# Layer 0 of a two-layer kernel: the second and third weight load of layer 1 issued by ScalarE behind the norm, and the queries' PSUM evictions moved from VectorE to ScalarE

## Chip, cores and metric

One Trainium2 chip, one core. The metric is the device time of one execution in microseconds (us). Engines: PE is TensorE (matrix multiplies; PEld is its weight load), DVE is VectorE, ACT is ScalarE, POOL is GpSimd, SP is SyncE, which here does nothing but ask for transfers. Each engine works through its own instructions in the order in which they were issued and waits on semaphores for the others. PE writes its results into eight PSUM banks, from which DVE or ACT must fetch ("evict") them before the bank can be used again. A transfer (DMA) is asked for by an instruction in one engine's order and carried out by 16 DMA engines beside all of that.

## What is computed

Two layers on x of 4 batches, 256 tokens, 512 features, float32. Each layer norms x and adds an attention-like and a feed-forward branch to it. The change lies in layer 0:

```python
def _L0_attn_ref(x, ...):            # 32 heads, 4 latent numbers a head
    C_q = x @ Wq_d + bq_d            # 512 -> 12
    C_kv = x @ Wkv_d + bkv_d         # 512 -> 4
    q = (C_q @ W_qk + b_qk).reshape(b, s, 32, 4)
    scores = jnp.einsum('bqhd,bkd->bhqk', q, C_kv) / jnp.sqrt(4)
    attn = jax.nn.softmax(scores, axis=-1)
    V = (C_kv @ Wv_u + bv_u).reshape(b, s, 32, 16)
    ...
    return out @ Wo + bo

def _L0_ffn_ref(x, W_gate, W_up, W_down):      # M = 1792
    h = silu(x @ W_gate.T) * (x @ W_up.T)
    return h @ W_down.T

x = x + _L0_attn_ref(xn, ...) + _L0_ffn_ref(xn, ...)
```

Layer 1 norms the new x and adds a selective scan (its input projection `in_proj_w` is 512 x 2048) and a routed feed-forward.

## The kernel before

The order of the work is written out by hand. The feed-forward of layer 0 is a generator (`gate_up`, then `down`): each `yield` is one small step of matmuls, and `go(ff, n)` lets n steps of it run. The attention's steps are called between such `go`s, so that PE has feed-forward matmuls to do while DVE and ACT work on the attention. Tokens go in two halves `th` of 512 (batches 0 and 1, then 2 and 3).

**Feed-forward.** `gate_up(th)` goes over 14 blocks m of 128 hidden features. For each it asks, through GpSimd's queue (L427), for the 256 KB of weights needed three steps on (`wgu`, four buffers), and makes `pg` (gate) and `pu` (up) by 8 matmuls each (L444), since x is held as a high and a low part (`xhi`, `xlo`). ACT makes tanh of `pg` (L451), DVE makes `g` from it (L452) and multiplies by `pu` (L454), ACT rounds that to `hhi` (L455), GpSimd makes the rest `hlo` (L456). `down(th, i)` adds up one block of 128 output tokens in the bank `po`: first the attention's part (L464), from `o8n` and `m_att`, then the hidden features (L469).

**Queries.** `latents(b)` is a generator run for batches 0 and 1 together, later for 2 and 3. It makes the latent numbers of q and k, then `pq`, the queries of 128 (head, latent) rows by 2 x 256 (L310), which is evicted with bias and factor into `q` (L314), rounded to `qhi` by ACT (L319); DVE makes the rest `qlo` (L320). Then 4 times `pqg` by a selection matrix (L335), evicted into `qg` (L337). `scores_max` makes trial scores `sc` (L352) from `qg` and keys `km`, and DVE takes their row maxima `mpl` (L354) out of PSUM. Later `attend` makes exponentials and `weigh` sums them into `av`.

**Norm.** `normalize(b)` copies the sums out of `av` as `o8` (ACT), spreads the denominators over the rows in the bank `pden` (L407), and in four pieces takes the reciprocal (L413) and multiplies (L414) into `o8n`, all on DVE.

**PSUM.** `pg`, `pu`, `po`, `pq`, `pqg`, `pden` take turns in the banks of one pool, so each waits until the one before it in the same bank was read.

**End of layer 0.** After the attention of batch 3 the pool `we` is opened. `w_in` has three buffers of 512 KB for layer 1's input projection; the helper `weights` (L619 to L621) asks SP for such a load. The first is asked for when the pool opens, then `vec`, and two more in the loop over the pieces of `normalize(3)`, which are interleaved with the last two hidden blocks. SP has nothing else to do there and waits for nothing. These loads are for L753 (`px`, layer 1). After `go(ff)` the last `down`s follow, and layer 1 begins.

Of the kernel before, what the change touches and what calls it, by code (L numbers as in the profile page):

```python
# [8 lines left out]
F32 = mybir.dt.float32  # L9

F32R = mybir.dt.float32r
AF = mybir.ActivationFunctionType
ALU = mybir.AluOpType
# [4 lines left out]
P = 128  # L18
# [4 lines left out]
NH, KVL, QL = 32, 4, 12  # L23
# [18 lines left out]
def block_kernel(  # L42
# [24 lines left out]
    nc = tc.nc  # L67
# [5 lines left out]
    x = keep.tile([P, NTB, D], F32, name="x")  # L73
# [28 lines left out]
    ap1 = att.enter_context(tc.tile_pool(name="att", bufs=1, side="right"))  # L102
# [6 lines left out]
    blat = ap1.tile([P, 3], F32, name="blat")  # L109
# [24 lines left out]
    selk = ap1.tile([40, P], F32R, name="selk")  # L134
    ks = ap1.tile([40, S], F32R, name="ks")
    mask = ap1.tile([P, 8], F32, name="mask")


    zk = ap1.tile([P, NTB, 56], F32, name="zk")
# [2 lines left out]
    for i in range(2):  # L142
        t = ap1.tile([P, 2, 4, 32], F32, name=f"mpl{i}")
# [23 lines left out]
    def masks():  # L167
        nc.vector.tensor_reduce(
            mask, ident.rearrange("p (h r) -> p r h", h=4)[:, 16:24, :], AX.X, ALU.add
        )  # L170
        nc.vector.tensor_scalar_mul(mask, mask, -1.0)

    def fold_load():
        live["wvt"] = ffn.tile([P, 4, P], F32, tag="g", name="wvt", bufs=2)
        nc.sync.dma_start(live["wvt"], wvt_d)
        live["wo"] = ap1.tile([P, 4, D], F32, tag="pe", name="wo", bufs=2)
        nc.sync.dma_start(live["wo"], wo_d)
        nc.sync.dma_start(bo, bo_d)
# [107 lines left out]
    def latents(b):  # L286

        xnT = tok[b // 2][0][:, :, b % 2 * S : (b % 2 + 1) * S]
        pl = psmm.tile([P, 2, S], F32, tag="mm", name="pl")
        for hc in range(HC):  # L290
            mm(pl[:40, 0, :], lhsT=wlat[:, hc, :], rhs=xnT[:, hc, :],
               start=(hc == 0), stop=(hc == HC - 1))
        kT = ap1.tile([8, S], F32, tag="kT", name="kT")
        nc.scalar.activation(kT, pl[32:40, 0, :], AF.Identity, bias=blat[32:40, 2:3])
        nc.scalar.copy(ks[0:8, :], kT)
        nc.vector.tensor_tensor(ks[32:40, :], kT, ks[0:8, :].bitcast(F32), ALU.subtract)
        cq = ap1.tile([P, 512], F32, tag="rd", name="cq")[:QL, 0:S]
        nc.scalar.activation(cq, pl[:QL, 0, :], AF.Identity, bias=wqk[:, 0:1])
        yield
        yield  # L300

        kms[b] = ap1.tile([P, S], F32R, tag="km", name="km", bufs=2)
        p = psmm.tile([P, S], F32, tag="mm", name="pkm")
        mm(p, lhsT=selk, rhs=ks, start=True, stop=True)
        nc.scalar.copy(kms[b], p)
        yield
        pq = psmm.tile([P, 2, S], F32, tag="mm", name="pq")
        q8 = ap1.tile([P, 2, S], F32, tag="q8", name="q8")
        for hf in range(2):
            mm(pq[:, hf, :], lhsT=wqk[:, 1 + hf * P : 1 + (hf + 1) * P], rhs=cq,  # L310
               start=True, stop=True)
        for hf in range(2):

            nc.vector.tensor_scalar(  # L314
                q8[:, hf, :], pq[:, hf, :], blat[:, hf : hf + 1], 1.0 / KVL**0.5,
                ALU.add, ALU.mult,
            )
        part = [ap1.tile([P, 2, S], F32R, tag=f"q{n}", name=f"q{n}") for n in ("hi", "lo")]
        nc.scalar.copy(part[0], q8)  # L319
        nc.vector.tensor_tensor(part[1], q8, part[0].bitcast(F32), ALU.subtract)  # L320
        yield


        pz = psmm.tile([P, 2, P], F32, tag="mm", name="pz")
        for i in range(2):
            mm(pz[:, i, :], lhsT=kT[:, i * P : (i + 1) * P], rhs=ident[0:8, :], start=True, stop=True)
        nc.vector.tensor_copy(zk[:, 2 * b : 2 * b + 2, 24:32], pz[:, :, 0:8])
        yield
        qg = ap1.tile([P, 4, 2, S], F32R, tag="qg", name="qg", bufs=2)
        qs[b] = qg  # L330
        for gq in range(4):
            p = psmm.tile([P, 2, S], F32, tag="mm", name="pqg")
            for hf in range(2):
                for k in range(2):
                    mm(p[:, hf, :], lhsT=selq[:, gq, 4 - 4 * k : 4 - 4 * k + P],  # L335
                       rhs=part[k][:, hf, :], start=(k == 0), stop=(k == 1))
            (nc.scalar.copy if gq % 2 else nc.vector.tensor_copy)(qg[:, gq], p)  # L337
            yield


# [60 lines left out]
    def normalize(b):  # L401

        o8 = ffn.tile([P, 2, S], F32, tag="o8", name="o8")
        nc.scalar.copy(o8, avs[b])
        yield
        pd = psmm.tile([P, 2, S], F32, tag="mm", name="pden")
        mm(pd.rearrange("p a b -> p (a b)"), lhsT=rep, rhs=o8.rearrange("p a b -> p (a b)"),  # L407
           start=True, stop=True)
        rd = ffn.tile([P, 2, S], F32, tag="rd", name="rd")
        yield  # L410
        for i in range(4):
            w = slice(i * S // 4, (i + 1) * S // 4)
            nc.vector.reciprocal(rd[:, :, w], pd[:, :, w])  # L413
            nc.vector.tensor_tensor(  # L414
                o8ns[b // 2][:, :, b % 2 * S + i * S // 4 : b % 2 * S + (i + 1) * S // 4],
                o8[:, :, w], rd[:, :, w], ALU.mult,
            )
            yield
# [11 lines left out]
    def gate_up(th):  # L430


        hi, lo = hids[th]
        xs = tok[th][1]
        for m in range(MC):
            for k in range(2):
                i = th * NW + 2 * m + k
                load_w(i + 3)
                if th == 0 and k == 0 and m % 2 == 1:
                    nc.gpsimd.dma_start(wd[:, m - 1 : m + 1, :], wd_d[:, m - 1 : m + 1, :])  # L440
                ps = psmm.tile([P, 512], F32, tag="mm", name="pg" if k == 0 else "pu")
                for hc in range(HC):
                    for j in range(2):
                        mm(ps, lhsT=wgus[i][:, hc, :], rhs=xs[j][:, hc, :],  # L444
                           start=(hc == 0 and j == 0), stop=(hc == HC - 1 and j == 1))
                    if hc < HC - 1:
                        yield

                if k == 0:
                    g = ffn.tile([P, 512], F32, tag="g", name="g", bufs=2)  # L450
                    nc.scalar.activation(g, ps, AF.Tanh, scale=0.5)  # L451
                    nc.vector.scalar_tensor_tensor(g, g, 1.0, ps, ALU.add, ALU.mult)  # L452
                else:
                    nc.vector.scalar_tensor_tensor(g, g, 0.5, ps, ALU.mult, ALU.mult)  # L454
                    nc.scalar.copy(hi[:, m, :], g)  # L455
                    nc.gpsimd.tensor_tensor(lo[:, m, :], g, hi[:, m, :].bitcast(F32), ALU.subtract)  # L456
                yield

    def down(th, i):

        tb = 4 * th + i
        po = psmm.tile([P, D], F32, tag="mm", name="po")
        for hf in range(2):
            mm(po, lhsT=o8ns[th][:, hf, i * P : (i + 1) * P], rhs=m_att[:, hf, :],  # L464
               start=(hf == 0), stop=False)
        yield
        for m in range(MC):
            for j in range(2):
                mm(po, lhsT=hids[th][j][:, m, i * P : (i + 1) * P], rhs=wd[:, m, :],  # L469
                   start=False, stop=(m == MC - 1 and j == 1))  # L470
            if m < MC - 1 or th:
                yield
        if tb < 5:
            nc.vector.tensor_tensor(x[:, tb, :], x[:, tb, :], po, ALU.add)
        else:
            live["last", tb] = po
        yield
# [5 lines left out]
    def go(gen, n=1000):  # L483
        for _ in range(n):
            if next(gen, 1) == 1:
                break
# [64 lines left out]
    ff = gate_up(0)  # L551
# [22 lines left out]
    norm = normalize(0)  # L574
# [7 lines left out]
    norm = normalize(1)  # L582
    next(norm)
    go(ff)
    ff = (0 for i in range(4) for _ in down(0, i))
# [22 lines left out]
    ff = gate_up(1)  # L608
    attention(2, ff, True, 6)
    norm = normalize(2)  # L610
# [5 lines left out]

    we = ctx.enter_context(tc.tile_pool(name="we", bufs=1, side="right"))

    def weights(d, c0):  # L619
        t = we.tile([P, 2, HC, P], F32, tag="w_in", name="w_in", bufs=3)  # L620
        nc.sync.dma_start(t, d[:, c0 : c0 + 2])  # L621
        return t

    w_of = {("x", 0, 0): weights(inx_d, 0)}
# [5 lines left out]
    norm = normalize(3)  # L630
    next(norm)
    go(ff, 4)
    for i, _ in enumerate(norm):
        go(ff, 2)
        if i in (1, 3):
            w_of["x", 0, i // 2 + 1] = weights(inx_d, i + 1)
    go(ff)
    ffs.close()
    ps0.close()

# [40 lines left out]
    for i in range(2):  # L681
        t = w1.tile([P, 2, KC - 1 + S], F32, name=f"pad{i}")
# [421 lines left out]
    ff = (0 for i in range(4) for _ in down(1, i))  # L1104
# [18 lines left out]
    for i in range(2):  # L1123
        v = vec[:, 6 + i, :]
        nc.scalar.activation(px[:, i, :], px[:, i, :], AF.Identity, bias=v[:, V_CB : V_CB + 1],
                             scale=v[:, V_CW + KC - 1 : V_CW + KC])
# [341 lines left out]
```

## Time and profile before

| | us |
|---|---|
| runs | 854.57, 855.86, 847.67, 852.38 (median 853.47) |
| the profiled execution | 852.83 |
| its span (first to last instruction) | 851.1 |
| mean granted clock of PE | 0.952 of full |
| one up or down step's matmul on PE (L444 `pu`) | 0.427 |
| score maxima on DVE (L354) | 1.219 each, 64 of them |
| norm's reciprocal on DVE (L413) | 0.950 each, 16 of them |
| one `wgu` load, 256 KB, from issue to landing | 2.7 (median) |
| one `w_in` load, 512 KB, from issue to landing | 4.4 (median) |

The page has the span in 40 equal slices of 21 us; each digit is an engine's busy share in tenths.

```profile
PE   5999999989999999989787889887898997956875
DVE  4687755377754435798799999899999999999996
ACT  4325575223556367599876789876888885855561
POOL 3223321001333432669958689869599859697664
```

Layer 0 is the first 14 or 15 slices, layer 1 the rest. A row of a timeline is: start, duration, engine, line, operation, output <- inputs, shape of the output <- of the input, count; in brackets how long the engine was idle ahead of it and what ended that.

### The profile page before, as it was taken

The numbers are of one execution on the slowest core, as the hardware profiler recorded it, in microseconds if no ns is written. First come the engines' busy times: TensorE is split into PE (matmuls) and PEld (weight loads), VectorE is DVE, ScalarE is ACT, GpSimd is POOL, SyncE is SP. The second block draws the span as 40 slices with busy tenths as digits, with TensorE's granted clock in tenths as the row PEclk, the third lists the DMA queues.
The fourth block names the chain that finished last, engine by engine and source line by source line (L and its number), as shares of the span: only waits on it lengthen the run. The fifth ranks groups of instructions, "written<-read, shape, count | busy, mean of one in ns | idle before, by whom it ended". The sixth has DMA issues, their size and how long they took to land.

```text
span 851.1 us, 10982 instructions
## 1 busy us (share of the span) xinstructions
PE 741.9 (87%) x3798; PEld 423.9 (50%) x3798; DVE 670.1 (79%) x647; ACT 538.5 (63%) x1061; POOL 488.9 (57%) x376
## 2 busy tenths in 40 slices
PE   5999999989999999989787889887898997956875
PEld 3565546656555676657444346344356444312331
DVE  4687755377754435798799999899999999999996
ACT  4325575223556367599876789876888885855561
POOL 3223321001333432669958689869599859697664
PEclk9999999979999999999898999989999979998998
DMA  7224322001222322555651644433553343443400
GB/s 222 78 84 125 93 81 62 0 1 38 75 75 75 116 56 63 135 151 161 201 146 50 173 128 134 123 99 107 154 159 100 101 112 102 109 122 102 112 25 25
DMA packets 67202, 86.71 MB, mean 102 GB/s; under 512 B 12061, under 2 KB 52009, under 8 KB 66762
## 3 DMA queue, kind: packets, MB, share of 16 engines
q1 hardware_dynamic: 57786, 67.12, 27.9%
q0 software_dynamic: 9072, 18.35, 7.7%
q8 instruction: 30, 0.49, 0.2%
q10 hardware_dynamic: 288, 0.52, 0.2%
q14 instruction: 26, 0.21, 0.1%
HBM read 66.58 MB, written 10.22 MB: 90 GB/s over the span
## 4 chain that ended last, share of the span: by engine, by line
PE 37%; DVE 31%; POOL 11%; ACT 10%; issue 6%; DMA 4%; SPq 1%; DVEq 0%; POOLq 0%; ACTq 0%
DVE h L979 19%; POOL hc L984 6%; PE pg L444 6%; DVE bx L964 6%; PE pu L444 6%; ACT decay L958 6%; PE av L397 4%; PE po L469 4%; PE scT L386 2%; PE px L753 2%; DVE mpl L354 2%; DMA dus<-dud 2%; PE po L1088 2%; PE po L464 1%; PE pp L809 1%
## 5 line engine op out<-in xcount | busy, mean ns | idle before, releaser
L984 POOL TENSOR_TENSOR hc<-h,cr 128x1024 f32<-128x1024 f32 (+1 forms) x130 | 301.6, 2322 | 95.0 <-DVE h L979 77.4
L979 DVE TENSOR_TENSOR_SCAN h<-decay,bx 128x1024 f32<-128x1024 f32 (+1 forms) x129 | 288.0, 2234 | 16.2 <-PE po L469 3.9
L958 ACT ACTIVATE decay<-dts,aneg 128x255 f32<-128x255 f32 x504 | 213.3, 498 | 96.2 <-DVE h L979 85.9
L964 DVE TENSOR_TENSOR bx<-brow,dus 128x1024 f32<-128x1024 f32 x128 | 157.7, 1232 | 9.1 <-DMA dus<-dud 5.0
L996 PE MATMUL ysum<-hc,stack 128*32 128x256 f32 x1024 | 88.3, 414 | 59.3 <-POOL hc L984 59.1
L456 POOL TENSOR_TENSOR hlo<-g,hhi 128x512 fp32r<-128x512 f32 x28 | 35.9, 1282 | 116.5 <-ACT hhi L455 116.5
L427 POOL DMA_DIRECT2D wgu<-in_wgu x56 | 31.1, 556 | 100.6 <-PE pg L444 98.0
L354 DVE TENSOR_REDUCE mpl<-sc 128x4 f32<-128x1024 f32 x64 | 76.6, 1219 | 13.2 <-PE sc L352 13.0
L996 PEld LDWEIGHTS ysum<-hc,stack 128*32 128x32 f32 x1024 | 21.2, 111 | 119.8 <-POOL hc L984 98.4
L388 ACT ACTIVATE pe<-scT 128x1024 f32<-128x1024 f32 x64 | 64.0, 1023 | 23.4 <-PE sc L352 16.8
L1088 PE MATMUL po<-ow,xc 128*128 128x512 f32 x128 | 69.2, 649 | 2.2 <-DVE xc L1000 2.2
L926 PE MATMUL pz<-xn1T,w_in 128*128 128x256 f32 x256 | 68.1, 413 | 0.0
L753 PE MATMUL px<-xn1T,w_in 128*128 128x256 f32 x256 | 61.8, 387 | 0.1
L926 PEld LDWEIGHTS pz<-xn1T,w_in 128*128 128x128 f32 x256 | 49.4, 202 | 19.4 <-issue 11.5
L753 PEld LDWEIGHTS px<-xn1T,w_in 128*128 128x128 f32 x256 | 48.2, 192 | 13.1 <-issue 4.3
L452 DVE SCALAR_TENSOR_TENSOR g<-g,pg 128x512 f32<-128x512 f32 x28 | 19.2, 686 | 41.5 <-ACT g L451 41.5
L469 PE MATMUL po<-wd,hhi 128*128 128x512 f32 x112 | 51.1, 456 | 0.0
L444 PE MATMUL pu<-xhi,wgu 128*128 128x512 f32 x112 | 47.9, 427 | 1.8 <-DMA wgu<-in_wgu 1.8
L444 PE MATMUL pg<-xhi,wgu 128*128 128x512 f32 x112 | 49.1, 438 | 0.0
L455 ACT CAST hhi<-g 128x512 fp32r<-128x512 f32 x28 | 17.3, 619 | 47.5 <-DVE g L454 47.5
L469 PE MATMUL po<-wd,hlo 128*128 128x512 f32 x112 | 45.4, 405 | 0.0
L444 PE MATMUL pu<-xlo,wgu 128*128 128x512 f32 x112 | 44.8, 400 | 0.0
(230 smaller groups left out, 1252.6 us busy)
## 6 DMA issues: line engine op xcount, KB each, us to landing
dts<-dtd SPq DMA_DIRECT2D x124, 128.0 KB, 2.9
dus<-dud SPq DMA_DIRECT2D x124, 128.0 KB, 2.9
wgu<-in_wgu POOLq DMA_DIRECT2D x56, 256.0 KB, 2.7
w_in<-in_inx SPq DMA_DIRECT2D x16, 512.0 KB, 4.4
w_in<-in_inz SPq DMA_DIRECT2D x16, 512.0 KB, 4.6
dtd<-dt SPq DMA_DIRECT2D x15, 256.0 KB, 2.3
dud<-du SPq DMA_DIRECT2D x15, 256.0 KB, 2.3
wd<-in_wd POOLq DMA_DIRECT2D x7, 512.0 KB, 3.5
```

The lines of the kernel that those rows point to most:

```text
L354: nc.vector.tensor_reduce(mpl2[b % 2][:, qb, 2 * hp : 2 * hp + 2, 16 + 2 * gq : 18 + 2 * gq], sc.rearrange("p i (f k) -> p i f k", f=2), A ...
L388: nc.scalar.activation(pes[b, k][:, 2 * t : 2 * t + 2, :], sc, AF.Exp)
L444: mm(ps, lhsT=wgus[i][:, hc, :], rhs=xs[j][:, hc, :], start=(hc == 0 and j == 0), stop=(hc == HC - 1 and j == 1))
L469: mm(po, lhsT=hids[th][j][:, m, i * P : (i + 1) * P], rhs=wd[:, m, :], start=False, stop=(m == MC - 1 and j == 1))
L753: mm(px[:, i, :], lhsT=w[:, i, hc, :], rhs=xns[b][:, hc, :], start=(hc == 0), stop=(hc == HC - 1))
L926: mm(pz[:, i, :], lhsT=w[:, i, hc, :], rhs=xns[b][:, hc, :], start=(hc == 0), stop=(hc == HC - 1))
L958: nc.scalar.activation(da[:, k, 1:], live["dts", b, c][:, k, 1:], AF.Exp, scale=aneg[:, c, k, g : g + 1])
L964: nc.vector.tensor_tensor(bx, brow[g // 2][:, g % 2, :].unsqueeze(1).to_broadcast([P, NG, S]), live["dus", b, c], ALU.mult)
L979: nc.vector.tensor_tensor_scan(h[:, n].rearrange("p n t -> p (n t)"), da[:, n].rearrange("p n t -> p (n t)"), bx[:, n].rearrange("p n t -> ...
L984: (nc.vector if k == NG - 1 else nc.gpsimd).tensor_tensor(hc[:, n], h[:, n], crows[b][:, g, :].unsqueeze(1).to_broadcast([P, NG // parts, ...
L996: mm(ysum[k * NB : (k + 1) * NB, :], lhsT=stack, rhs=hc[:, k, :], start=False, stop=(g == NU - 1))
L1088: mm(live["po", b, i], lhsT=xcs[b][:, c, i * P : (i + 1) * P], rhs=late_w["ow"][:, c, :], start=False, stop=(c == DC - 1))
```

## The change

Three things, all in layer 0:

- `weights` takes the engine that asks as an argument. The second and third `w_in` load are no longer asked for in the loop over `normalize(3)` but behind it: the first of them when the loop has ended, the other four steps of `gate_up` later, both by ACT. The steps of `gate_up` and of `normalize` keep their order.
- `q` is evicted by two ACT operations (bias and factor) in the place of two DVE operations, in each batch. Their bias is a new tile `bhalf`, the bias already multiplied by the factor, made once by one small DVE operation in `masks`.
- All four `qg` evictions of a batch are ACT's; so far DVE had the two even ones. DVE loses 8 operations of L314 and 8 of L337 and gains one; ACT gains 16 and two DMA issues. The orders of the other operations are as before.

```diff
@@ masks()
         nc.vector.tensor_scalar_mul(mask, mask, -1.0)
+        nc.vector.tensor_scalar_mul(bhalf, blat[:, 0:2], 1.0 / KVL**0.5)
@@ latents(b)
         for hf in range(2):
-            nc.vector.tensor_scalar(
-                q8[:, hf, :], pq[:, hf, :], blat[:, hf : hf + 1], 1.0 / KVL**0.5,
-                ALU.add, ALU.mult,
-            )
+            nc.scalar.activation(q8[:, hf, :], pq[:, hf, :], AF.Identity,
+                                 bias=bhalf[:, hf : hf + 1], scale=1.0 / KVL**0.5)
...
-            (nc.scalar.copy if gq % 2 else nc.vector.tensor_copy)(qg[:, gq], p)
+            nc.scalar.copy(qg[:, gq], p)
@@ end of layer 0
-    def weights(d, c0):
+    def weights(d, c0, eng=nc.sync):
         t = we.tile([P, 2, HC, P], F32, tag="w_in", name="w_in", bufs=3)
-        nc.sync.dma_start(t, d[:, c0 : c0 + 2])
+        eng.dma_start(t, d[:, c0 : c0 + 2])
         return t
...
-    for i, _ in enumerate(norm):
+    for _ in norm:
         go(ff, 2)
-        if i in (1, 3):
-            w_of["x", 0, i // 2 + 1] = weights(inx_d, i + 1)
-    go(ff)
+    for p in (1, 2):
+        w_of["x", 0, p] = weights(inx_d, 2 * p, nc.scalar)
+        go(ff, 4 if p == 1 else 1000)
```

More of the change, by code (lines that the diff above doesn't have):

```diff
@@ L136, in block_kernel @@
     mask = ap1.tile([P, 8], F32, name="mask")
+    bhalf = ap1.tile([P, 2], F32, name="bhalf")
     zk = ap1.tile([P, NTB, 56], F32, name="zk")
```

## The prediction

> **What bounds the kernel now.** I read the page's head first, to see which engine fills which stage.
>
> ```profile
> span 851.1 us, 10982 instructions
> PE 741.9 (87%) x3798; PEld 423.9 (50%) x3798; DVE 670.1 (79%) x647; ACT 538.5 (63%) x1061; POOL 488.9 (57%) x376
> PEclk9999999979999999999898999989999979998998
> ```
>
> The third line is the clock granted to TensorE (PE), one digit for each 21 us. Layer 0 is the first 14 slices, where PE is 9 tenths busy; the whole change lies there. The scan of layer 1, which VectorE (DVE) fills, is untouched. So only what shortens or lengthens PE's path before about 300 us counts, and busy time taken off DVE is worth nothing by itself.
>
> Then the chain of waits at the norm of the last batch, and the timeline there.
>
> ```profile
> 283.63 5.40 DMA wgu<-in_wgu
> 289.17 2.09 PE pu L444 x8
> 291.26 1.08 PE po L464 x2
> ```
>
> ```profile
> 281.32 0.90 SPq L621 DMA_DIRECT2D w_in<-in_inx  x2
> ...
> 287.38 0.68 DVE L454 SCALAR_TENSOR_TENSOR g<-g,pu 128x512 f32<-128x512 f32 x1
> 287.98 0.95 DVE L413 RECIPROCAL rd<-pden 128x128 f32<-128x128 f32 x1
> ...
> 288.96 1.26 DVE L414 TENSOR_TENSOR o8n<-o,rd 128x128 f32<-128x128 f32 x1
> ...
> 289.17 0.47 PE L444 MATMUL pu<-xhi,wgu 128*128 128x512 f32 x1 [1.81 <-DMA wgu<-in_wgu]
> ...
> 290.15 0.94 DVE L413 RECIPROCAL rd<-pden 128x128 f32<-128x128 f32 x1
> ...
> 291.21 0.30 PEld L464 LDWEIGHTS po<-m_att,o8n 128*128 128x128 f32 x2 [0.39 <-issue]
> 291.24 1.95 PE L464 MATMUL po<-m_att,o8n 128*128 128x512 f32 x4
> ```
>
> The last gate/up weights need 5.40 us (the page's median for such a load is 2.7), because three w_in loads of 512 KB share the DMA engines, and PE stands 1.81 us for them. That is what part 1 could win. Beside it DVE works without a gap from 284.39 to 292.81, and po starts right behind the fourth reciprocal (290.15+0.94=291.09), since po takes the PSUM bank that pden held. Then the windows: first three of PE alone (stretch, its us, PE's busy time and count, granted clock, DMA share, GB/s), then one of all engines (PE, PEld, DVE, ACT, POOL) at the loads, where the transfers are full.
>
> ```profile
> 22.40:24.00 1.60, 0.62 (x4) 1.00 0.57 160
> 48.80:51.20 2.40, 1.55 (x13) 1.00 0.80 248
> 52.00:56.00 4.00, 4.00 (x18) 0.57 0.23 66
> ```
>
> ```profile
> 284.00:286.00 2.00, 2.00 (x10) 1.65 (x9) 1.58 (x3) 0.36 (x1) 0.20 (x1) 1.00 1.01 342
> ```
>
> Last the queries of the second batch, where DVE's order holds PE:
>
> ```profile
> 46.17 0.88 DVE L314 TENSOR_SCALAR q<-pq,blat 128x256 f32<-128x256 f32 x2 [0.43 <-PE pq L310]
> 47.08 0.62 ACT L319 CAST qhi<-q 128x512 fp32r<-128x512 f32 x1 [1.48 <-DVE q L314]
> 47.73 0.69 DVE L320 TENSOR_TENSOR qlo<-q,qhi 128x512 fp32r<-128x512 f32 x1 [0.68 <-ACT qhi L319]
> 48.33 2.35 DVE L354 TENSOR_REDUCE mpl<-sc 128x4 f32<-128x1024 f32 x2
> ...
> 56.39 0.68 DVE L337 CAST qg<-pqg 128x512 fp32r<-128x512 f32 x1
> ```
>
> q, qhi, qlo and mpl follow each other with under 0.05 us between; PE's scores wait for mpl (0.63 us at 50.74).
>
> **Part 1, the two w_in loads.** They are taken off SP at 281.3 and put on ScalarE's (ACT's) queue behind the norm: the first between g and hhi of the last hidden block, the second after that hhi. ACT idles 3.64 us ahead of that hhi (292.85) and from 293.47 to 300.41; two issues there cost what two loads cost to issue in the first row above, 0.90 us, all inside idle time, with nothing but that hhi queued behind. SP's two issues go, at no gain: SP had nothing late.
> What it frees: the last wgu, asked for at 283.63, would land by the median 2.7 at 286.3, before PE wants it (287.36). Then pu is released by DVE: its bank was read by L454, which ends at 287.38+0.68=288.06. So pu starts near 288.15 and not 289.17: 1.02 us. But po still waits for the fourth reciprocal, which DVE's gapless row of work puts at 291.09 whenever pu comes. The matmuls of pu are then finished at 290.3, and PE waits there 0.8 to 1 us in place of here. What is late next is DVE. Gain 0 if DVE keeps its pace; L414 took 1.26 us where its other three of this norm took 0.29, beside a GpSimd subtract, and might lose a little of that. I take -0.05; bounds 0 and -1.0, or -1.8 if neither bank held PE.
> What it risks: the loads land later. w_in takes 4.4 us by the page's median, 5.8 at the longest; asked for at about 289.2 and 293.5 they land by 295.0 and 299.3, and layer 1 reads them at 300.78 and 304.81. At least 5.5 us are spare.
>
> [...]
>
> **Part 2, q on ACT.** DVE's pair of tensor_scalar takes 0.88. This kernel has no such instruction on ACT out of pq; the nearest row is L791, the same 128x256 out of PSUM with a bias pointer, 0.467 us; where two such follow each other (L853 and L854 at 324.58 and 324.95) they start 0.37 apart, so a pair is 0.84. The dear end is L768, with bias and scale pointers: 0.554, or 1.10 for two that don't overlap. So -0.04 to +0.22 in each of four batches; I take L791, since scale is a constant here: 4 x -0.04 = -0.16; bounds -0.2 and +0.9. All of it is on the path, since qhi, qlo and mpl hang on it, but DVE gains nothing between: it must still pass qlo before mpl. ACT has 1.48 idle us ahead of qhi at 47.08, so nothing is queued behind a wait there. The new bhalf is one 128x2 DVE operation in an idle stretch at 15.7 to 18.2: nothing.
>
> **Part 3, qg on ACT.** Eight casts go from DVE (689 ns) to ACT (587 ns, with 18.5 us idle ahead of its eight). 5.5 us leave DVE, but the next DVE work mostly waits for something else: after 56.39 mpl could start 0.5 earlier, yet the g behind it waits for ACT's g (59.19) and the next mpl for PE's sc (59.41). The others are alike, at 194.86 with 0.17 us of room. I take -0.04, bounds 0 and -0.2.
>
> Sum: -0.05-0.16-0.04=-0.25 on the profiled execution of 852.83 (span 851.1): 852.58. The median shown, 853.47, is 0.64 above that execution, so 853.2 us.
>
> **Rivals.** 1, *the stall passes through*: DVE's end is not what holds po (its weights' row says issue), and PE's 1.81 us at 287.36 go. For it: the chain runs from the wgu load to po without a DVE step. Against: 291.09 and 291.21 are too close. Price -1.0 to -1.8, and with fewer pauses one stretch of half clock may go, which is (1-0.57) x 4.00=1.7 us by the third window row: 852.83-0.25-1.0-1.7=849.9, or 850.5 as a median.
> 2, *the slower side, ACT's pair is dear and the clock answers*. The pair is 1.10, +0.9 in all; PE's pause behind mpl at 50.74 grows by 0.22, and pauses move to other places (part 1 moves one to 290.3). In the window rows a stretch with PE busy 1.55 of 2.40 was followed by a clock of 0.57, while 0.62 of 1.60 was not; the whole trace of layer 0 loses (1-0.57) x 24=10.3 us in such stretches (52 to 56, 158 to 162, 174.4 to 182.4, 188 to 196). One more: 852.83+0.9+1.7=855.4, as a median 856.1; two more, 857.8. It decides from the first pause that tips; five more stretches of 4 us would be 8.5 us, 1%.
> 3, *a w_in load is late*: each us past the 5.5 spare costs one; against it, the DMA share is near nothing there after wgu ends. 855 at 2 us late.
>
> [...]
>
> **How the numbers follow.** About 1%, 8.5 us, is what a measurement of this kernel can tell from no change (the four runs lie between 847.67 and 855.86). Forecast, no change, 0.62, all within 1%. Rival 1, 0.15, of it 0.06 beyond 1%, where several half-clock stretches go with the stall. Rival 2, 0.20, of it 0.11 beyond 1%. Rival 3, 0.03, within. So faster 0.06, same 0.83, slower 0.11. The range takes rival 1 with 1.8 us and a stretch and some spread of the runs (848) and rival 2 with two more half-clock stretches (858).
>
> **What would show it.** Part 1: the last wgu back at some 2.7 us and pu near 288.15, and, if I am right, a new pause of nearly a us ahead of po; po starting a us earlier against its L452 neighbours makes rival 1 right. Part 2: a row of L314 on ACT near 0.47 and qhi 0.84 behind its start; 0.55 is rival 2. Part 3: DVE idle growing by what left it. The clock's windows tell the rest: stretches of 0.57 that come or go make me wrong, either way, more than any term of the sum.

## The result and the profile after

The changed kernel has a median of 854.9 us (54 runs, 849.83 to 860.57), the kernel before 853.06 us beside it (78 runs, 846.33 to 856.62). The ratio is 1.0027 with a 95% interval of 1.0012 to 1.0042: a small loss, well within the 1% and within the range, but on the other side of the forecast, which was a quarter of a microsecond less and not two more. One run of e3_qg below fell in a slower state, 1.6% above the fastest of its kernel, and is left out of the means.

The head of the page of the changed kernel, its profiled execution being 856.74 us:

```profile
span 855.0 us, 10983 instructions
PE 750.8 (88%) x3798; PEld 426.5 (50%) x3798; DVE 664.8 (78%) x632; ACT 546.1 (64%) x1077; POOL 488.9 (57%) x376
PEclk9999999889999999999888999978999978988996
```

DVE has lost 15 instructions and 5.3 us of work, ACT has gained 16 and 7.6. PE's busy time has gone up by 8.9 us with the same 3798 matmuls: they ran at a lower granted clock (0.938 over the span, 0.952 before). That is where one would look first, but in layer 0 there is no loss to explain: po of the last norm starts at 288.44 us here and at 291.24 before. The span is 3.9 us longer all the same, so this execution loses 6.7 us behind that po, nearly all of it in layer 1, whose program the change does not touch.

The timeline of the changed kernel at the last norm (start, duration, engine, line, idle time before and what ended it):

```profile
285.17 0.95 DVE L413 RECIPROCAL rd<-pden 128x128 f32<-128x128 f32 x1
285.30 0.50 PE L444 MATMUL pu<-xhi,wgu 128*128 128x512 f32 x1 [0.81 <-DVE g L454]
285.38 0.33 ACTq L621 DMA_DIRECT2D w_in<-in_inx  x1
...
286.15 1.27 DVE L414 TENSOR_TENSOR o8n<-o,rd 128x128 f32<-128x128 f32 x1
...
287.35 0.94 DVE L413 RECIPROCAL rd<-pden 128x128 f32<-128x128 f32 x1
...
288.44 1.96 PE L464 MATMUL po<-m_att,o8n 128*128 128x512 f32 x4 [1.03 <-DVE rd L413]
...
290.05 0.34 ACTq L621 DMA_DIRECT2D w_in<-in_inx  x1
```

The wait for wgu is gone. In the place of 1.81 us ahead of pu there are 0.81 (DVE's read of the bank) and a new one of 1.03 ahead of po: 1.84 in all. The reciprocals run through as they did.

The queries of the second batch in the changed kernel:

```profile
46.12 0.84 ACT L316 ACTIVATE q<-pq,bhalf 128x256 f32<-128x256 f32 x2 [0.56 <-PE pq L312]
46.99 0.62 ACT L319 CAST qhi<-q 128x512 fp32r<-128x512 f32 x1
```

```profile
47.64 0.69 DVE L320 TENSOR_TENSOR qlo<-q,qhi 128x512 fp32r<-128x512 f32 x1 [1.95 <-ACT qhi L319]
48.25 1.22 DVE L354 TENSOR_REDUCE mpl<-sc 128x4 f32<-128x1024 f32 x1
```

The pair takes 0.84, and q to mpl 2.13 us where it was 2.16.

### The profile page after: what moved, and what is told of

The parts are those of the page before. It is cut to its first block, busy times and chain, and to the rows that moved or that the text cites. A ratio compares the mean times of both kernels' runs of the same rounds, so it can differ in the third digit from the quotient of the medians.

```text
span 855.0 us, 10983 instructions
## 1 busy us (share of the span) xinstructions
PE 750.8 (88%) x3798; PEld 426.5 (50%) x3798; DVE 664.8 (78%) x632; ACT 546.1 (64%) x1077; POOL 488.9 (57%) x376
## 4 chain that ended last, share of the span: by engine, by line
PE 40%; DVE 26%; ACT 12%; POOL 12%; issue 6%; DMA 2%; SPq 1%; DVEq 0%; POOLq 0%; ACTq 0%
DVE h L981 15%; POOL hc L986 7%; PE pg L444 6%; ACT decay L960 6%; PE pu L444 5%; DVE bx L966 4%; PE av L397 4%; PE po L469 3%; DVE mpl L354 3%; PE po L1090 2%; PE px L755 2%; PE scT L386 2%; POOL xc L797 2%; PE ysum L998 2%; PE pz L928 2%
## 5 line engine op out<-in xcount | busy, mean ns | idle before, releaser
L998 PE MATMUL ysum<-hc,stack 128*32 128x256 f32 x1024 | 91.4, 427 | 53.5 <-POOL hc L986 53.3
L1090 PE MATMUL po<-ow,xc 128*128 128x512 f32 x128 | 72.2, 674 | 2.2 <-DVE xc L1002 2.2
L928 PE MATMUL pz<-xn1T,w_in 128*128 128x256 f32 x256 | 71.0, 427 | 0.0
L928 PEld LDWEIGHTS pz<-xn1T,w_in 128*128 128x128 f32 x256 | 51.3, 210 | 21.3 <-issue 12.2
L444 PE MATMUL pg<-xlo,wgu 128*128 128x512 f32 x112 | 44.4, 396 | 0.0
```

Source lines behind the costliest of these rows:

```text
L444: mm(ps, lhsT=wgus[i][:, hc, :], rhs=xs[j][:, hc, :], start=(hc == 0 and j == 0), stop=(hc == HC - 1 and j == 1))
L928: mm(pz[:, i, :], lhsT=w[:, i, hc, :], rhs=xns[b][:, hc, :], start=(hc == 0), stop=(hc == HC - 1))
L998: mm(ysum[k * NB : (k + 1) * NB, :], lhsT=stack, rhs=hc[:, k, :], start=False, stop=(g == NU - 1))
L1090: mm(live["po", b, i], lhsT=xcs[b][:, c, i * P : (i + 1) * P], rhs=late_w["ow"][:, c, :], start=False, stop=(c == DC - 1))
```

## The experiments

Times are device microseconds; "mean" is over the runs of a kernel, and "error" is a standard error. Each group of kernels ran beside the kernel before, each group on a different chip, and the mean of before is not the same in each (851.92 beside the parts, 851.64 beside the delays, 853.27 beside the last three kernels). So "over before" is always against the runs of before in the same group. The changed kernel has 854.66 in 54 runs and before 852.37 in the 78 beside it: 2.3 more, with an error of 0.6.

### The parts alone

e1_dma is the kernel before with only the loads moved, e2_q with only q's eviction (and bhalf), e3_qg with only this line, e4_evict with both evictions:

```diff
-            (nc.scalar.copy if gq % 2 else nc.vector.tensor_copy)(qg[:, gq], p)
+            nc.scalar.copy(qg[:, gq], p)
```

> Only the two w_in loads moved to ACT; q and qg evicted as before. Clock theory (the change's own path is no longer than before; what moved the median is how many half-clock stretches of PE an execution meets, and where in the span they lie): the last wgu lands in under 3.5 us, PE's 1.81 us wait ahead of pu shrinks to 0.8 and a new wait of 1.0 stands ahead of po, as in the profile after; the medians differ by what the mean clock differs, anything from -3 to +3 us, and spans at an equal mean clock agree with those of before within 0.5 us. Rival, loads (the later w_in loads or ACT's part in asking for them cost layer 1 something): the ratio is that of the whole change, 1.002 to 1.004, and at an equal clock the spans are 2 us longer.

> Only q's eviction moved to ACT with the new bhalf; qg and the loads as before. Clock theory: 0.04 us less per batch on the path, the median differs by the clock alone, from -3 to +3 us. Rival, path (an ACT eviction costs PE time in layer 0): median 1 to 2 us longer and the start of the last norm's po later by 1 us or more at an equal number of half-clock stretches before it.

> Only the even qg evictions moved to ACT; q and the loads as before. Clock theory: under 0.2 us on the path, the median differs by the clock alone, from -3 to +3 us. Rival, path: median 1 to 2 us longer at an equal clock.

> Both evictions moved, the loads as before, that is, the change without its loads. If the parts add up, its difference is that of q alone plus that of qg alone, and the loads make the rest to +2 us. Clock theory: the parts need not add up, since each moves the later work against the clock's stretches by tenths of a microsecond; PE's 1.81 us wait ahead of pu is back.

| kernel | runs | mean | over before (error) | ratio, 95% |
|---|---|---|---|---|
| e1_dma | 12 | 852.27 | +0.3 (0.9) | 1.0009 (0.9983 to 1.0035) |
| e2_q | 12 | 854.83 | +2.9 (1.0) | 1.0034 (1.0002 to 1.0066) |
| e3_qg | 11 | 856.01 | +4.1 (1.1) | 1.0047 (1.0015 to 1.0078) |
| e4_evict | 12 | 853.62 | +1.7 (1.1) | 1.0017 (0.9991 to 1.0044) |

e1_dma shows the wait move as foretold; its chain into po consists of DVE steps and ends with the reciprocal (start, duration, what):

```profile
285.21 0.88 DVE rd L413
286.09 0.02 issue
286.11 1.27 DVE o8n L414
287.38 0.88 DVE rd L413
288.26 0.14 issue
288.40 1.96 PE po L464 x4
```

In e3_qg, with the loads on SP, the same chain has `DMA wgu<-in_wgu` with 6.27 us. The loads are therefore not what costs; the evictions are suspect, although both together come out dearer than before by less than either alone. A cost on a path would not do that, but the errors are of the size of these differences. The runs scatter by some 10 us, and most of that goes with the clock: over the 54 runs of the changed kernel the span and the PE time lost by a lowered clock (one minus the mean clock, times the span) correlate with 0.94, at 0.39 us of span for each lost one. My theory at this point was that the change shifts work against the clock's stretches, though e3_qg lies outside the 3 us that I had given it for that.

### Layer 0 alone

If the evictions cost time where they stand, layer 0 by itself must show it. These kernels run it several times over in one execution, so that the clock's lot is drawn more often:

```diff
+def block_kernel(tc, *args):
+    with tc.manual_schedule():
+        for _ in range(3):
+            layer0(tc, *args)
...
+    for i in range(4):
+        go(down(1, i))
+    for tb in range(5, NTB):
+        add_last(tb)
+    for tb in range(NTB):
+        nc.sync.dma_start(out_d[tb * P : (tb + 1) * P, :], x[:, tb, :])
```

> Layer 0 of the kernel before alone, three times over in one execution, and x written out behind each; layer 1 is left out (its w_in and vec loads stay). It is the base for the next two. Some 3 x 315 us; three draws of the half-clock stretches in each execution.

> The same of the changed kernel. If the change costs its 1.8 us in layer 0 (more half-clock stretches there, or a longer path), the mean span is 3 to 6 us over l0_before. If layer 0 is as foretold, -0.25 us each, and what moved lies in layer 1, the mean span is within 1.5 us of l0_before or below it.

> The same with the two loads moved and the evictions as before. If the loads only move the wait from pu to po, 0 to -0.3 us against l0_before; if the shorter single pause also saves a half-clock stretch in some executions, down to -1.5 us in three layers. If the evictions are what costs in layer 0, l0_after is over this one by 2 to 6 us.

Six runs each: means 988.20, 976.23 and 976.19, so 4.0 us for each layer in favour of the moved loads. That is not the change's doing but a flaw of these kernels: SP, which waits for nothing there, asked for four stores of x right behind the w_in loads, and PE's wait grew with them. In l0_before:

```profile
290.52 0.47 PE L443 MATMUL pu<-xhi,wgu 128*128 128x512 f32 x1 [4.21 <-DMA wgu<-in_wgu]
```

It shows what the part would be worth where the wait is longer than DVE's reciprocals, 4.21 us in the place of 1.81: then it goes through to the end. With the stores asked for by GpSimd behind its last subtract, and five layers:

> Layer 0 of the kernel before alone, five times over, layer 1 left out. As l0_before, but the stores of x are asked for by GpSimd behind its last subtract, so that they no longer share the transfers with the last wgu (there that made PE's wait 4.21 us in the place of 1.81). PE's wait ahead of the last pu is 1.5 to 2.2 us in each of the five.

> The same with the two loads moved. If DVE's reciprocal catches all of it, the mean span is within 1 us of l0b_before in five layers; if the shorter pause also saves half-clock stretches, 1.7 us for each saved, 1 to 5 us in five layers.

> The same with q and qg on ACT, the loads as before. If the evictions are what makes the changed kernel 1.8 us slower, 5 to 12 us over l0b_before in five layers. If layer 0 is as foretold, -0.2 us each, -1 in five, with the clock's stretches for scatter, within 3 us.

> The same of the whole change: the sum of the two above. If it is not slower than l0b_before, the 1.8 us of the whole kernel do not come from layer 0's work but from where layer 1 falls.

| kernel | mean of 6 runs | against l0b_before, for one layer (error) |
|---|---|---|
| l0b_before | 1628.69 | |
| l0b_dma | 1624.73 | -0.8 (0.4) |
| l0b_evict | 1629.62 | +0.2 (0.4) |
| l0b_after | 1627.93 | -0.15 (0.4) |

So layer 0 does what was foretold, and two us are not lost there. In the profiles of l0b_before and l0b_evict 3 of the 10 layers have a stretch of lowered clock right behind the wait for wgu (in l0b_before pu's matmuls take 0.63 us there in two layers, 0.40 in the other three), in l0b_dma and l0b_after none of 10. That is the likely source of l0b_dma's 0.8, though twice its error reaches nought.

### Layer 1 shifted

If the loss is in layer 1 and comes from where it falls against the clock, a plain delay between the layers must do the like. d4, d8 and d12 add 4, 8 and 12 matmuls to the kernel before, and e3b_qg is the dearest part again, to see whether it was scatter.

```diff
     go(ff)
+    dl = pssc.tile([P, 2, 512], F32, tag="sc", name="dl")
+    for _ in range(4):
+        mm(dl[:, 0, :], lhsT=hids[1][0][:, 0, 0:P], rhs=wd[:, 0, :], start=True, stop=True)
     ffs.close()
```

> The kernel before with 4 more matmuls on PE (into a bank that nobody reads) between layer 0 and layer 1, some 0.9 us, that move layer 1 against the rest and change nothing else. If an execution meets the clock's 3.41 us windows at a place that is drawn at random, the mean is that of before plus 0.9. If the start of the execution is tied to these windows, so that moving layer 1 by a part of one changes which of its pauses cost clock, the three means of d4, d8 and d12 do not follow the delay: some of them lie 2 us or more off the line, either way.

> As d4 with 8 matmuls, some 1.8 us. At random: before plus 1.8. Tied: off that by 2 us or more in one of the three.

> As d4 with 12 matmuls, some 2.8 us. At random: before plus 2.8. Tied: off that by 2 us or more in one of the three; 2.8 is near the 3.41 us of a window, so that it may be back at before plus 2 to 3.

> e3_qg once more (only the even qg evictions on ACT), since its mean was 4 us over before although layer 0 alone shows no such cost. If that was the scatter of twelve runs, the mean is within 1.5 us of before. If it is a property of the kernel (work of layer 1 that falls badly, or a cost that the trace has not shown), it is 3 us or more over before again.

| kernel | runs | mean | over before (error) | delay put in |
|---|---|---|---|---|
| d4 | 12 | 853.14 | +1.5 (0.7) | 0.9 |
| d8 | 12 | 855.28 | +3.6 (1.1) | 1.8 |
| d12 | 12 | 855.89 | +4.2 (0.8) | 2.8 |
| e3b_qg | 12 | 855.95 | +4.3 (0.6) | |

No delay lies 2 us off the line, which was the sign set for the clock, but all three lie above it, by 0.6 to 1.8 us with errors of 0.7 to 1.1. So this test speaks against the theory of the clock and does not rule out that moving layer 1 costs something. The stronger sign is that e3_qg is dear again, by as much: the clock makes scatter, but this loss belongs to the kernel.

The profiles then gave it away. Layer 1's scan has units of 3.69 us each, some of which have additional work; the table has the time from one scan's start to the next, in us, from the timelines' rows of the scan (unit 0 is the first whole scan). The instructions of DVE are those of the compiled program, waits included; the traces have two rows fewer in each.

| kernel | DVE's instructions in the program | unit 82 | unit 83 | unit 84 | unit 86 | second ex |
|---|---|---|---|---|---|---|
| before | 896 | 4.25 | 3.83 | 3.66 | 8.42 | 0.19 |
| e1_dma | 896 | 4.25 | 3.84 | 3.65 | 8.42 | 0.19 |
| d8 | 896 | 4.24 | 3.84 | 3.65 | 8.43 | 0.19 |
| e2_q | 888 | 4.05 | 6.06 | 4.01 | 8.43 | 2.31 |
| e3_qg | 888 | 4.04 | 6.06 | 4.01 | 8.42 | 2.32 |
| e3b_qg | 888 | 4.04 | 6.06 | 4.01 | 8.42 | 2.33 |
| e4_evict | 880 | 4.04 | 6.05 | 3.66 | 8.58 | 2.33 |
| after | 880 | 4.04 | 6.06 | 3.65 | 8.58 | 2.31 |

In d4 and d12 these units are as in d8. The profiled executions of before and the changed kernel differ in layer 1 by more than unit 83: unit 19 takes 3.81 and 6.06 us, unit 54, where DVE waits for PE's `ysum`, 4.43 and 6.07, and from the last scan's start to the end it is 8.5 and 10.7 us, at a mean clock of 0.99 and 0.67. But each of these three takes both values among the kernels with 896 instructions; unit 83 takes one value with 896 and another in all the others of this table.

In unit 83 lies the route of the second pair of batches: ACT copies the logits ml, DVE takes their maximum (m) and subtracts it (ex). Here is that place in the kernel before,

```profile
679.67 0.40 DVE L1000 TENSOR_TENSOR xc<-ysum,sz 128x256 f32<-128x256 f32 x1
680.21 2.29 DVE L979 TENSOR_TENSOR_SCAN h<-decay,bx 128x1024 f32<-128x1024 f32 x1
...
681.95 0.29 ACT L1013 COPY ml<-pr 128x136 f32<-128x136 f32 x1
...
682.41 0.16 DVE L1035 TENSOR_REDUCE m<-ml 128x4 f32<-128x32 f32 x1
...
682.60 0.19 DVE L1036 TENSOR_TENSOR ex<-ml,m 128x32 f32<-128x32 f32 x1
682.64 2.38 POOL L984 TENSOR_TENSOR hc<-h,cr 128x1024 f32<-128x1024 f32 x1 [1.89 <-PE ysum L996]
682.71 1.23 DVE L964 TENSOR_TENSOR bx<-brow,dus 128x1024 f32<-128x1024 f32 x1
```

and in the changed one:

```profile
678.95 0.41 DVE L1002 TENSOR_TENSOR xc<-ysum,sz 128x256 f32<-128x256 f32 x1
679.28 2.27 DVE L981 TENSOR_TENSOR_SCAN h<-decay,bx 128x1024 f32<-128x1024 f32 x1
...
681.24 0.29 ACT L1015 COPY ml<-pr 128x136 f32<-128x136 f32 x1
...
681.56 0.19 DVE L1037 TENSOR_REDUCE m<-ml 128x4 f32<-128x32 f32 x1
681.69 2.35 POOL L986 TENSOR_TENSOR hc<-h,cr 128x1024 f32<-128x1024 f32 x1 [1.66 <-DVE h L981]
681.78 2.31 DVE L1038 TENSOR_TENSOR ex<-ml,m 128x32 f32<-128x32 f32 x1
...
684.01 1.22 DVE L966 TENSOR_TENSOR bx<-brow,dus 128x1024 f32<-128x1024 f32 x1
```

GpSimd's hc starts 0.14 us behind the end of the scan in both. The subtract starts 0.10 behind it before the change and is done; after it, 0.23, which is 0.09 behind GpSimd, and this subtract of 32 numbers a partition then takes as long as hc, to within 0.05 us of its end. bx, behind it in DVE's order, is 2.2 us late, and so is each later scan. The kernel before had 0.04 us to spare.

The rows beside GpSimd's work differ by where the kernel keeps the operands. ex reads ml and m, both in SBUF, and took 2.31 us behind hc's start, 0.19 ahead of it; o8n (L414) reads two SBUF tiles and took 1.26 to 1.28 us in the four of its sixteen that stood beside hlo, 0.29 in the other twelve, in both traces. bx reads brow from PSUM and takes 1.23 us beside hc as alone; the scan reads bx, which lies in PSUM here, and takes 2.29 beside hc as alone. By what means GpSimd holds ex and o8n is not shown.

What sets the 0.13 us apart is the unit before. With 896 instructions in DVE's program unit 82 takes 0.2 us more, and the scan behind it starts 0.14 us after the operation in front of it (680.21 against 679.67+0.40); in the changed kernel it overlaps with that operation (679.28 against 678.95+0.41). ACT does not share this delay: ml starts 2.28 and 2.29 us behind xc's start. So before the change ml is there 0.25 us ahead of the scan's end, m overlaps with that end and the subtract follows; after it ml ends 0.02 us ahead of the scan's end, m starts only 0.03 behind ml, and the subtract comes too late.

With 8 instructions fewer a delay of 0.35 us sits in unit 84, with 16 fewer one of 0.16 in unit 86. It keeps its place in DVE's program: in the traces' rows of DVE, waits included and counted from 0, it is row 703 in every kernel. This row starts 0.40 us behind the end of the row before it with 896 and 888 instructions and 0.19 with 880, where 0.03 to 0.05 or an overlap is usual. So it moves through the work when instructions are taken off in layer 0.

### The position, tested

f1_pad16 brings the changed kernel back to 896, f2_pad8 takes the kernel before to 904, both with memsets of a small unused tile in layer 0; f3_route puts the subtract elsewhere.

```diff
         nc.vector.tensor_scalar_mul(mask, mask, -1.0)
+        for _ in range(16):
+            nc.vector.memset(idle, 0.0)
@@ f3_route
         nc.vector.tensor_reduce(m1, lg, AX.X, ALU.max)
+
+    def route_sub(b):
+        lg = live["ml"][:, :, 0:NE]
         nc.vector.tensor_tensor(ex, lg, over(m1), ALU.subtract)
         nc.scalar.activation(ex, ex, AF.Exp)
...
-                put(b, 22, route_exp, b)
+                put_late(b, 21, route_exp, b)
+                put_late(b, 22, route_sub, b)
```

> The changed kernel with 16 memsets of a 128x2 tile on DVE in layer 0, where DVE idles. They bring DVE's program back to the 896 instructions that it had before (880 after), so that every instruction of layer 1 lies again where it lay in DVE's program. Theory, position: the profiles of all kernels with an eviction moved (880 or 888 instructions) have the route's subtract (ex) of the second pair of batches 0.1 us behind GpSimd's start on hc and take 2.3 us for it in the place of 0.19, those with 896 do not, as a delay of some 0.2 us in the unit before, which sits at a fixed place of DVE's program, sets them apart. So here: ex 0.19 us at the second place, unit 83 back at 3.8 us from 6.06, the delayed unit (4.25 us) back at 82, and a mean 2.2 us below the changed kernel, that is, within 1.2 us of before. Rival, evictions: what ACT took over keeps the cost; unit 83 stays at 6.06 and the mean at 2.3 over before.

> The kernel before, nothing moved, with 8 such memsets, so that DVE's program has 904 instructions. Position: the delayed unit moves from 82 to 80, nothing holds the subtract back any more, unit 83 takes 6.06 us, and the mean is some 2 us over before. Rival, evictions: as before within 1 us, unit 83 at 3.8.

> The changed kernel with the route's subtract put one unit later, directly behind a scan, so that it starts before GpSimd's next hc, and its maximum left where it was. Collision theory: ex 0.19 us at both places, unit 83 back at 3.8, and a mean 2 to 3.5 us below the changed kernel (the first place collides in some executions too). If the subtract is not what costs, the mean stays within 1 us of the changed kernel.

| kernel | unit 82 | unit 83 | mean of 12 | over before (error) | ratio, 95% |
|---|---|---|---|---|---|
| f1_pad16 | 4.25 | 3.84 | 851.24 | -2.0 (0.7) | 0.9977 (0.9956 to 0.9998) |
| f2_pad8 | 4.05 | 6.07 | 854.64 | +1.4 (1.2) | 1.0016 (0.9983 to 1.0049) |
| f3_route | 4.04 | 3.71 | 850.85 | -2.4 (0.8) | 0.9969 (0.9942 to 0.9995) |

The same place in f1_pad16, f2_pad8 and f3_route, one fence each:

```profile
677.03 0.16 DVE L1040 TENSOR_REDUCE m<-ml 128x4 f32<-128x32 f32 x1
...
677.23 0.19 DVE L1041 TENSOR_TENSOR ex<-ml,m 128x32 f32<-128x32 f32 x1
677.26 2.38 POOL L989 TENSOR_TENSOR hc<-h,cr 128x1024 f32<-128x1024 f32 x1 [1.89 <-PE ysum L1001]
```

```profile
678.23 2.36 POOL L987 TENSOR_TENSOR hc<-h,cr 128x1024 f32<-128x1024 f32 x1 [1.67 <-DVE h L982]
678.32 2.33 DVE L1039 TENSOR_TENSOR ex<-ml,m 128x32 f32<-128x32 f32 x1
```

```profile
681.32 0.17 DVE L1041 TENSOR_TENSOR ex<-ml,m 128x32 f32<-128x32 f32 x1
681.44 1.23 DVE L966 TENSOR_TENSOR bx<-brow,dus 128x1024 f32<-128x1024 f32 x1
681.55 2.35 POOL L986 TENSOR_TENSOR hc<-h,cr 128x1024 f32<-128x1024 f32 x1 [1.38 <-DVE ex L1041]
```

Sixteen memsets that compute nothing take the changed kernel from 2.3 us over before to 2.0 under it and take the collision away; eight of them give the kernel before the collision, unit 83 at 6.07, which is the surer reading, since its time alone would not settle it. The forecast that f2_pad8's delay moves to unit 80 missed: row 703 has its 0.40 us there too, but it is now a wait that passes while a scan runs, and no unit grows by it. With the subtract put directly behind a scan it comes ahead of hc although the program has 880 instructions, and that version is 2.4 us faster than before.

The sizes fit less well than the places. Unit 83 is worth 2.2 us; f1_pad16 gained 4.3 (error 0.9) and f3_route 4.7 (1.0) on the changed kernel, and e3_qg and e3b_qg lost more than 4. What makes the rest is not shown.

There is a second collision, at the route of the first pair of batches. In the profiles it falls either way: ex is held for 1.3 to 1.6 us in e1_dma, d4, d8, d12, e4_evict and the changed kernel, where unit 19 takes 6.06 or 6.07 us; ex takes 0.19 in before, e2_q, e3_qg, e3b_qg, f1_pad16 and f2_pad8, where unit 19 takes 3.81 or 3.82. In the changed kernel DVE had waited 0.99 us for a late ml there. In f3_route it is not there either (0.17 us). One execution of each kernel was profiled, so how often it falls in the others is not known, and it may be part of that rest.

## Why the prediction was wrong

**The wait of 1.81 us, part 1: right in kind, small in size.** It was to go from pu to po, pu to start at the bank's release, po behind the fourth reciprocal, with a pause of 0.8 to 1 us; it was 0.81 ahead of pu and 1.03 ahead of po. The size, 0.05, was that of an execution in which the clock does not answer: in 3 of 10 layers it did, and the average may be 0.8 (l0b_dma, error 0.4). If that is real, rival 1's price came in by the clock, not by the stall. The loads show no cost of being late: e1_dma's mean is that of before within 0.9 us. One reading was wrong and cost nothing: ACT is not idle from 293.47, since a table load of 1.28 us (L704) stands there.

**Part 2: right in its rows; part 3: too small to see.** ACT's operation took 0.471 us and the pair 0.84, as the rows taken had it (L791, L853), and qhi starts 0.03 behind it. For layer 0 the sum said -0.25 us; l0b_after has -0.15 with an error of 0.4, which agrees and could not tell it from nought.

**What failed is a sentence ahead of the sum:** "The scan of layer 1, which VectorE (DVE) fills, is untouched. So only what shortens or lengthens PE's path before about 300 us counts". The scan's instructions are untouched, but their place in DVE's program is not: it has 16 fewer ahead of them. That took away a delay of 0.2 us in unit 82 that had let the route's subtract start ahead of GpSimd, and the subtract then stood 2.1 us behind hc, on DVE, which bounds layer 1 (busy for 396.1 of the 415 us from 425 to 840 in before). f1_pad16 gives back the place with operations that compute nothing, and the loss is gone. None of the rivals had this, and rival 2, the slower side, had the wrong mechanism: the pair was not dear, and stretches of half clock scatter the runs rather than part the kernels. Its price for a stretch was too high as well: it took each lost us of PE's time for one of span, and over the 54 runs it is 0.39.

The trace of before had the warning. The prediction read o8n's 1.26 us beside a subtract of GpSimd, and priced it in its place only. Looking for other DVE operations with two SBUF inputs, as o8n has, close to a start of GpSimd's would have found ex, 0.04 us ahead of hc, on the path of the engine that bounds the second half. That the change would move it by 0.13 us, no row of before could tell.

**The range and the chance of a change within 1%** held, by luck: 854.9 lies between 848 and 858, but what moved it is in none of the terms and rivals that the range was made of.

## What to carry to other kernels

Where an engine's order of work is unchanged, its times need not be: here 16 instructions fewer ahead of it moved the rest of DVE's through its program, and a subtract that had 0.04 us to spare fell behind the start of GpSimd's hc and took 2.31 us in the place of 0.19. So before a stage is called untouched, look in it for operations that only just miss a conflict, here DVE's with two SBUF inputs (ex, o8n) near the start of a long GpSimd one (hc, 2.35 us), and put them directly behind the operation that both wait for, where ex took 0.17 us in f3_route. When the parts of a change don't add up and a part alone is dearer than the whole, compare the repeating units of the stages that were not touched, one by one, before the clock is blamed.

## What the runs showed of the hardware

**The lowered clock came in steps of 3.41 us.** In the profiled executions of before and of the changed kernel the granted clock is 1.00 or 0.50; the 16 and 18 stretches at 0.50 begin on a grid of 3.41 us and last one to three steps (3.41, 6.83 or 10.24 us; the last of each is cut off by the end). Counted from the first instruction, the grid lies 0.32 us later in the changed kernel's execution. The window rows of before on that grid (stretch, its us, PE busy and count, granted clock, DMA share, GB/s):

```profile
171.69:175.10 3.41, 2.13 (x13) 1.00 0.00 0
175.10:178.52 3.42, 3.42 (x15) 0.50 0.02 5
178.52:181.93 3.41, 3.41 (x6) 0.50 0.00 0
```

And the same work in the changed kernel, where the pause falls across two windows:

```profile
168.60:172.01 3.41, 2.71 (x19) 1.00 0.00 0
172.01:175.43 3.42, 2.79 (x19) 1.00 0.01 2
175.43:178.84 3.41, 3.41 (x19) 1.00 0.02 5
```

Here a window in which PE is busy for 2.13 of 3.41 us is followed by two at a clock of 0.50; the same pauses behind mpl (0.72 and 0.63 us there, 0.70 and 0.63 here), spread over windows of 2.71 and 2.79, are followed by one at 1.00. The busy time alone does not decide it: in before the window of the 1.81 us wait had less, 2.00, and the clock stayed at 1.00.

```profile
287.75:291.17 3.42, 2.00 (x8) 1.00 0.04 11
291.17:294.58 3.41, 3.41 (x12) 1.00 0.00 0
```

So the same pauses came ahead of no lowered clock in one execution and of 6.83 us at 0.50, 3.4 us of PE's time, in the other; layer 0 takes from DVE's first g<-g,pg to its last 265.2 to 265.9 us or 267.6 to 268.4 in the repeated layers of the l0b kernels' profiles, and single runs of one kernel lie 10 us apart. In the window at 171.69 pauses that add up to 1.3 us came ahead of a lowered clock, in the one at 287.75 pauses of 1.4 us did not, and which do so is not settled here.

**The delay at a fixed place of DVE's program** was not expected. That it moves with the number of instructions ahead is shown by three counts (880, 888, 896), and at 904 by row 703. It is not the only one: f2_pad8 has the same 0.40 us at rows 575 and 831, 128 rows ahead and behind, and its units 48 and 108 are 0.35 us longer by it. A load of program code is my guess: the page lists a DMA queue named "instruction", q14, with 26 packets and 0.21 MB, and in the trace one of its packets, of 8 KB, starts 0.7 to 1.2 us behind row 703 in every kernel that has 0.40 there, and 2.7 to 3.2 us behind it in the three with 880 instructions. No kernel was built to test it.
